# Three groups of tiles a round in a recurrence of layer norms and products, with results in single PSUM banks

## The chip, the cores and the metric

The kernel runs on one core of a Trainium2 chip. The metric is the time of one execution on the device, in microseconds (us). Three runs of the kernel before took 1946.14 to 1951.07 us, with a median of 1948.44. One further execution was recorded by the hardware profiler; every duration below is from that one.

The core's engines work side by side, each through its own list of instructions in order, and wait for one another by semaphores: TensorE (PE in the profile; PEld is its loading of weights), VectorE (DVE), ScalarE (ACT), GpSimd (POOL) and SyncE (SP), which issues DMAs. PE writes its results into PSUM. Its banks hold 512 float32 values a partition, and the kernel's pools use eight of them.

## The reference, cut to what matters

`x` has 3327 rows of 256 float32 features. Two layers follow each other, each a graph attention over a 3327 x 3327 adjacency and then a feed-forward part; every part takes a layer-normalized `x` and is added to `x`. The feed-forward part of layer 0 is a mixture of 16 experts, two of them for each row. That of layer 1 is a recurrence of 30 steps, and it is the part that the change touches:

```python
def step(h, _):
    h = h + 0.01 * jnp.tanh(h)
    h = h * jax.nn.sigmoid(h)
    h = _layernorm(h, ln_w, ln_b)
    h = jnp.einsum('bsc,dc->bsd', h, W) + b
    return (h, None)
x, _ = jax.lax.scan(step, x, None, length=N_ITERS)   # N_ITERS = 30
```

A row's next state depends on that row alone, and each step needs the one before.

## The kernel before, in words

The rows are held as 26 tiles of 128 rows in one SBUF tensor `x` (128 partitions x 26 x 256). The program has four stages: attention 0, whose products end at 391 us of the profile; the experts, from 395 us on; attention 1, whose products (L286) run from 793 to 1090 us; and the recurrence, whose first transpose is at 1090.1 us and whose last product starts at 1937.9 us. Results leave by DMA until the span ends at 1945.2 us.

In the recurrence the tiles form seven groups a step: six of four tiles and one of two. `x` holds the state times 100 (S). The layer norm is folded: `wc` is the weight matrix scaled by `ln_w`, with its mean taken out, so a product of the raw features gives the centred result; only the factor 1/sqrt(variance + eps) of each row (`rr`) is left to apply to the result, with the bias `bb`.

A list `parts` (L1080) has all 210 pairs of step and group in order. It is worked off in rounds of two parts (L1081 to L1084): first `turn_group` for both, then `next_state` for both.

`turn_group` (L1031): ScalarE computes tanh of a group's state (L1037, into `th`); GpSimd adds the state (L1039); ScalarE applies Silu (L1040, into `z`). For each tile VectorE takes the statistics (L1045), and PE transposes its two 128 x 128 halves (L1048) into a PSUM bank that holds two tiles (`pt`). The banks come from the pools `ps` and `ps_t` in turn, two banks each.

`next_state` (L1052): `inv_norm` (L1020) has VectorE aggregate the statistics (L1025) and GpSimd compute `rr` (L1027, L1028). ScalarE copies each bank of transposes to SBUF (L1058, `zT`). PE multiplies each tile with `wc`, two products a tile (L1063), into `po`, a PSUM tile for the whole group: 4 x 256 values, two banks; the pool has two such tiles, four banks. A second loop over the tiles has VectorE evict each one (L1069): result times `rr` plus `bb`, into `x`. In the last step a saved copy of the rows (`old`, from `kept`) is added (L1076) and the result goes out by DMA (L76).

What sets the order: transposes and products carry `tc.keep_in_program_order` and stand on PE as they are written. The rest of each engine's list is laid out by the framework's scheduler when the program is built, with the waits between engines set from the reads and writes of tiles; on the chip each list is followed in order. `th`, `z` and `zT` come from the pool `steps` with two buffers each; `stats`, `v` and `rr` from `small` with four.

Of the kernel before, what the change touches and what calls it, by code (L numbers as in the profile page):

```python
# [11 lines left out]
F32 = mybir.dt.float32  # L12
# [4 lines left out]
ALU = mybir.AluOpType  # L17
AX = mybir.AxisListType
PSUM = bass.MemoryType.PSUM

P = 128
# [4 lines left out]
G = 4  # L26
# [4 lines left out]
def gat_moe_gat_recurrent_ffn(ctx: ExitStack, tc: tile.TileContext, a: dict, out: bass.AP):  # L31
    nc = tc.nc
    N, D = a["x"].shape
# [30 lines left out]
    small = ctx.enter_context(tc.tile_pool(name="small", bufs=4))  # L64
# [3 lines left out]
    x = state.tile([P, NT, D], F32, name="x")  # L68
# [4 lines left out]
    def move_pairs(dram, tile, c0, c1, into_dram):  # L73

        def move(dst, src):
            nc.sync.dma_start(*((dst, src) if into_dram else (src, dst)))  # L76

        full = min(c1, PAIRS - 1)
        if full > c0:
            move(  # L80
                dram[c0 * 2 * P : full * 2 * P, :].rearrange("(t p b) d -> p t (b d)", p=P, b=2),
                tile[:, : 2 * (full - c0), :].rearrange("p (t b) d -> p t (b d)", b=2),
            )
        if c1 == PAIRS:
            base, last = (PAIRS - 1) * 2 * P, 2 * (PAIRS - 1 - c0)
            for r0, r1 in spread(REST // 2):
                move(
                    dram[base + 2 * r0 : base + 2 * r1, :].rearrange("(p b) d -> p (b d)", b=2),
                    tile[r0:r1, last : last + 2, :].rearrange("p b d -> p (b d)"),
                )  # L90
            if REST % 2:
                move(dram[base + REST - 1 : base + REST, :], tile[REST // 2 : REST // 2 + 1, last, :])
# [289 lines left out]
    with ExitStack() as moe:  # L382
# [5 lines left out]
        part = route_p.tile([P, 1], F32, name="part")  # L388
# [15 lines left out]
        ps = moe.enter_context(tc.tile_pool(name="ps0", bufs=4, space=PSUM))  # L404
        ps_o = moe.enter_context(tc.tile_pool(name="ps0o", bufs=2, space=PSUM))
# [240 lines left out]
        two = rec.tile([P, 2, SLOTS], F32, name="prod")  # L646
# [273 lines left out]
        wc = rec.tile([P, KD, D], F32, name="wc")  # L920
        bb = rec.tile([P, D], F32, name="bb")
# [15 lines left out]


    kept = dram.tile([NP, D], F32, name="kept")
    steps = ctx.enter_context(tc.tile_pool(name="steps", bufs=2))  # L940
    ps = ctx.enter_context(tc.tile_pool(name="ps2", bufs=2, space=PSUM))
    with ExitStack() as st:
        keep = st.enter_context(tc.tile_pool(name="keep2", bufs=1))
# [5 lines left out]
        ps_o = st.enter_context(tc.tile_pool(name="ps2o", bufs=2, space=PSUM))  # L949
# [62 lines left out]


    with ExitStack() as st:
        ps_t = st.enter_context(tc.tile_pool(name="ps3t", bufs=2, space=PSUM))
        turns = cycle((ps, ps_t))
        ps_o = st.enter_context(tc.tile_pool(name="ps3o", bufs=2, space=PSUM))
        last_p = st.enter_context(tc.tile_pool(name="last", bufs=2))

        def inv_norm(stats, n):  # L1020


            v = small.tile([P, G, 2], F32, name="v")
            for j in range(n):
                nc.vector.bn_aggr(v[:, j, :], stats[:, j, :])  # L1025
            r = small.tile([P, G], F32, name="rr")
            nc.gpsimd.tensor_scalar(r[:, :n], v[:, :n, 1], EPS, None, op0=ALU.add)  # L1027
            nc.gpsimd.tensor_tensor(r[:, :n], r[:, :n], neg_half[:, :n], ALU.pow)  # L1028
            return r

        def turn_group(ts):  # L1031

            n = len(ts)
            hs = x[:, ts[0] : ts[0] + n, :]
            th = steps.tile([P, G, D], F32, name="th")
            z = steps.tile([P, G, D], F32, name="z")
            nc.scalar.activation(th[:, :n, :], hs, AF.Tanh, scale=1.0 / S)  # L1037

            nc.gpsimd.tensor_tensor(th[:, :n, :], th[:, :n, :], hs, ALU.add)  # L1039
            nc.scalar.activation(z[:, :n, :], th[:, :n, :], AF.Silu, scale=1.0 / S)  # L1040
            stats = small.tile([P, G, 6], F32, name="stats")
            pool = next(turns)
            pt = [pool.tile([P, 2, KD, P], F32, name="bank") for _ in range(0, n, 2)]
            for j in range(n):
                nc.vector.bn_stats(stats[:, j, :], z[:, j, :])  # L1045
                for k in range(KD):
                    tc.keep_in_program_order(
                        nc.tensor.transpose(pt[j // 2][:, j % 2, k, :], z[:, j, k * P : (k + 1) * P], ident)  # L1048
                    )
            return pt, stats  # L1050

        def next_state(step, ts, pt, stats):  # L1052
            n = len(ts)
            hs = x[:, ts[0] : ts[0] + n, :]
            rr = inv_norm(stats, n)
            zT = steps.tile([P, G, KD, P], F32, name="zT")
            for c in range(n // 2):
                nc.scalar.copy(zT[:, 2 * c : 2 * c + 2, :, :], pt[c])  # L1058
            po = ps_o.tile([P, G, D], F32, name="po")
            for j in range(n):  # L1060
                for k in range(KD):
                    tc.keep_in_program_order(
                        nc.tensor.matmul(  # L1063
                            po[:, j, :], lhsT=zT[:, j, k, :], rhs=wc[:, k, :],
                            start=(k == 0), stop=(k == KD - 1),
                        )
                    )
            for j in range(n):
                nc.vector.scalar_tensor_tensor(  # L1069
                    x[:, ts[0] + j, :], po[:, j, :], rr[:, j : j + 1], bb, op0=ALU.mult, op1=ALU.add  # L1070
                )
            if step == N_STEPS - 1:
                here = slice(ts[0] * P, (ts[-1] + 1) * P)
                old = last_p.tile([P, G, D], F32, name="old")
                nc.sync.dma_start(old[:, :n, :], kept[here, :].rearrange("(t p) d -> p t d", p=P))
                nc.vector.scalar_tensor_tensor(hs, hs, 1.0 / S, old[:, :n, :], op0=ALU.mult, op1=ALU.add)  # L1076
                move_pairs(out, hs, ts[0] // 2, (ts[-1] + 1) // 2, True)


        parts = [(step, ts) for step in range(N_STEPS) for ts in groups]  # L1080
        for i in range(0, len(parts), 2):  # L1081
            two = [part + turn_group(part[1]) for part in parts[i : i + 2]]
            for part in two:
                next_state(*part)  # L1084


# [47 lines left out]
```

## Time and profile before

| | us |
|---|---|
| median of three runs | 1948.44 |
| profiled execution | 1946.91 |
| span of the profile, first to last instruction | 1945.2 |
| PE busy | 1899.3 |
| VectorE busy | 1278.6 |
| ScalarE busy | 1100.8 |
| GpSimd busy | 938.9 |
| products of the recurrence (L1063): 3120 passes, busy | 692.9 |
| transposes of the recurrence (L1048): 1560, busy | 187.7 |

The mean granted clock of PE is 0.994 of full speed.

How to read it. A line of the timeline has the start in us from the span's start, the time, the engine, the line of the kernel, the operation, output<-inputs, shapes and types, and how many instructions were merged (x32); in brackets stands the idle time of that engine just before and what ended it. A line of the costliest groups ends with the busy time of the group and the mean in ns of one, and behind the last bar the idle time ahead of the group. In the table of stretches each engine has its busy time and its number of instructions, and the last three columns are the granted clock of PE, the DMA share and the DMA rate. PE's products of float32 are two passes each, so 1560 products of the program stand as 3120. Passes are pipelined: the record of one overlaps the start of the next, so the pace is read from start to start. In a program's order, "waits DVE_49" on an instruction means that it waits for a count on VectorE's semaphore, "Activation_49" for one on ScalarE's.

### The profile page before, as it was taken

Reading aid. Unit: us, or ns where it says so; the run is one execution under the profiler, and the core shown is the slowest. Engines: PE = TensorE matmul, PEld = TensorE weight load, DVE = VectorE, ACT = ScalarE, POOL = GpSimd, SP = SyncE. Lnnn points to the kernel's source line nnn. Section 1 sums busy time; section 2 is a strip of 40 time slices with the busy share of each in tenths; the row PEclk is TensorE's granted clock in tenths of the full one; section 3 lists DMA queues with packets and bytes.
Section 4 is the critical chain, followed back from the end, with each engine's and each line's share of the span. In section 5 each row is a group of like instructions: output and inputs, shape, how many; then the busy total and the mean of one; then the engine's idle time right before and its main releaser. Section 6 shows DMA issues by size and latency. Waiting matters only on the chain.

```text
span 1945.2 us, 33722 instructions
## 1 busy us (share of the span) xinstructions
PE 1899.3 (98%) x11987; PEld 1745.9 (90%) x11987; DVE 1278.6 (66%) x3828; ACT 1100.8 (57%) x1593; POOL 938.9 (48%) x864
## 2 busy tenths in 40 slices
PE   7999999989999998999999999999999999999998
PEld 6999999989999996888888888888888888888887
DVE  6888788832222225477766777777777777777777
ACT  2977766721111112666655666666666666666664
POOL 3010202354333331001000488888888888888886
PEclk9999999999999998999999999999999999999999
DMA  8978051089999875000000100000000000000003
GB/s 170 120 104 116 10 86 51 18 295 292 350 336 335 290 249 174 9 21 13 18 20 11 36 1 1 1 1 1 1 1 1 1 1 2 1 1 1 1 1 119
DMA packets 140946, 158.61 MB, mean 82 GB/s; under 512 B 52168, under 2 KB 100555, under 8 KB 140777
## 3 DMA queue, kind: packets, MB, share of 16 engines
q1 hardware_dynamic: 124657, 123.57, 20.5%
q0 software_dynamic: 11440, 28.09, 8.4%
q10 hardware_dynamic: 4680, 4.76, 0.7%
q8 instruction: 98, 1.61, 0.3%
q14 instruction: 71, 0.58, 0.1%
HBM read 166.09 MB, written 29.80 MB: 101 GB/s over the span
## 4 chain that ended last, share of the span: by engine, by line
PE 72%; issue 9%; DVE 5%; POOL 5%; DMA 2%; ACT 0%; another core or an unknown queue 0%; SPq 0%; POOLq 0%; DVEq 0%; ACTq 0%
PE po L1063 35%; PE acc L286 23%; PE bank L1048 9%; POOL given L851 2%; DVE pT L281 2%; PE bank L831 2%; POOL rb L757 2%; DMA given<-wh,to 2%; PE acc L847 1%; PE acc L162 1%; PE bank L526 1%; POOL rstd L120 0%; PE bank L147 0%; DVE x L961 0%
## 5 line engine op out<-in xcount | busy, mean ns | idle before, releaser
L1063 PE MATMUL po<-wc,zT 128*128 128x256 f32 x3120 | 692.9, 380 | 0.0
L1063 PEld LDWEIGHTS po<-wc,zT 128*128 128x128 f32 x3120 | 585.3, 190 | 75.5
L1039 POOL TENSOR_TENSOR th<-th,x 128x1024 f32<-128x1024 f32 (+1 forms) x210 | 460.9, 2217 | 101.9 <-ACT th L1037 100.3
L276 ACT ACTIVATE e<-rb,minus,full 128x384 f32<-128x384 f32 (+3 forms) x494 | 400.4, 824 | 179.3 <-DVE pT L281 161.0
L281 DVE SCALAR_TENSOR_TENSOR pT<-e,part,adjT 128x384 f32<-128x384 f32 (+3 forms) x494 | 380.4, 774 | 131.9 <-PE acc L286 112.4
L1045 DVE BATCH_NORM_STATS2 stats<-z 128x6 f32<-128x256 f32 x780 | 273.9, 413 | 147.6 <-ACT z L1040 147.6
L1069 DVE SCALAR_TENSOR_TENSOR x<-po,rr,bb 128x256 f32<-128x256 f32 x780 | 321.0, 474 | 59.3 <-PE po L1063 57.5
L1058 ACT COPY zT<-bank 128x512 f32<-128x512 f32 x390 | 200.9, 599 | 270.2 <-PE bank L1048 270.2
L286 PE MATMUL acc<-wh,pT 128*128 128x129 f32 x2704 | 309.5, 276 | 1.6 <-DVE pT L281 1.6
L286 PEld LDWEIGHTS acc<-wh,pT 128*128 128x128 f32 x2704 | 305.0, 192 | 2.1 <-DVE pT L281 2.0
L286 PE MATMUL acc<-s_wh,pT 128*128 128x257 f32 x1352 | 296.1, 382 | 2.7 <-DVE pT L281 2.7
L286 PEld LDWEIGHTS acc<-s_wh,pT 128*128 128x128 f32 x1352 | 257.7, 191 | 40.9 <-DVE pT L281 4.8
L120 POOL TENSOR_TENSOR rstd<-ve,neg_half 128x4 f32<-128x4 f32 (+3 forms) x28 | 31.0, 1109 | 392.5 <-DVE ve L118 307.4
L1028 POOL TENSOR_TENSOR rr<-rr,neg_half 128x4 f32<-128x4 f32 (+1 forms) x210 | 209.2, 996 | 17.5
L1040 ACT ACTIVATE z<-th 128x1024 f32<-128x1024 f32 (+1 forms) x210 | 200.9, 1019 | 1.3 <-POOL th L1039 1.3
L1037 ACT ACTIVATE th<-x 128x1024 f32<-128x1024 f32 (+1 forms) x210 | 199.2, 1010 | 1.7 <-DVE x L127 1.7
L1048 PE MATMUL bank<-ident,z 128*128 128x128 f32 x1560 | 187.7, 273 | 1.6 <-DVE high L996 1.6
L1048 PEld LDWEIGHTS bank<-ident,z 128*128 128x128 f32 x1560 | 177.0, 141 | 12.4 <-ACT zT L1058 1.8
L881 DVE TENSOR_TENSOR pT<-e,bank 128x512 f32<-128x512 f32 x61 | 41.9, 687 | 183.2 <-PE bank L831 123.1
L831 PEld LDWEIGHTS bank<-hT,wh 128*128 128x128 f32 x1280 | 150.7, 194 | 8.3 <-ACT hT L823 6.4
L831 PE MATMUL bank<-hT,wh 128*128 128x128 f32 x1280 | 151.9, 278 | 5.8 <-ACT hT L823 5.8
L877 ACT ACTIVATE e<-bank 128x512 f32<-128x512 f32 x61 | 36.4, 597 | 189.6 <-issue 85.5
(192 smaller groups left out, 1331.7 us busy)
## 6 DMA issues: line engine op xcount, KB each, us to landing
wh<-in_w_dram SPq DMA_DIRECT2D x120, 512.0 KB
first_set<-in_w_dram SPq DMA_DIRECT2D x63, 512.0 KB
in_bytes<-in_adj_dram POOLq DMA_DIRECT2D x3, 2496.0 KB
x<-in_x_dram SPq DMA_DIRECT2D x6, 512.0 KB
kept<-x SPq DMA_DIRECT2D x8, 384.0 KB
old<-kept SPq DMA_DIRECT2D x6, 512.0 KB
out_dram<-x SPq DMA_DIRECT2D x6, 512.0 KB
table_x<-row ACTq DMA_DIRECT2D x3, 768.0 KB
```

The source lines that it names most:

```text
L276: nc.scalar.activation(e[:, : n * P], rb[:, : n * P], AF.Relu, scale=sc.full[:, j, h : h + 1], bias=sc.minus[:, j, h : h + 1],)
L281: masked = nc.vector.scalar_tensor_tensor(pT[:, : n * P], e[:, : n * P], sc.part[:, j, h : h + 1], adjT[:, j // 2, ts[0] * P : (ts[-1] + 1 ...
L286: nc.tensor.matmul(po[c], lhsT=pT[:, c * P : (c + 1) * P], rhs=wh[:, j, h, :], start=(j == 0 and c % per_bank == 0), stop=(j == NT - 1), s ...
L831: nc.tensor.matmul(p[:, f, :], lhsT=w[:, k, f * P : (f + 1) * P], rhs=hT[:, k, :], start=(k == 0), stop=(k == KD - 1),)
L1028: nc.gpsimd.tensor_tensor(r[:, :n], r[:, :n], neg_half[:, :n], ALU.pow)
L1039: nc.gpsimd.tensor_tensor(th[:, :n, :], th[:, :n, :], hs, ALU.add)
L1040: nc.scalar.activation(z[:, :n, :], th[:, :n, :], AF.Silu, scale=1.0 / S)
L1045: nc.vector.bn_stats(stats[:, j, :], z[:, j, :])
L1048: nc.tensor.transpose(pt[j // 2][:, j % 2, k, :], z[:, j, k * P : (k + 1) * P], ident)
L1058: nc.scalar.copy(zT[:, 2 * c : 2 * c + 2, :, :], pt[c])
L1063: nc.tensor.matmul(po[:, j, :], lhsT=zT[:, j, k, :], rhs=wc[:, k, :], start=(k == 0), stop=(k == KD - 1),)
L1069: nc.vector.scalar_tensor_tensor(x[:, ts[0] + j, :], po[:, j, :], rr[:, j : j + 1], bb, op0=ALU.mult, op1=ALU.add)
```

## The change

The recurrence takes three parts a round: three groups are turned, then all three have their products. 210 parts make 70 rounds. `steps` has three buffers; `ps_t` has four banks, and every second and third group takes its transposes' banks from it; `stats`, `v` and `rr` come from a pool `marks` of six. The results of the products go to PSUM tiles of two tiles, one bank each, of which there are two, and the eviction by VectorE stands in the same loop over the tiles as the products.

```diff
-    steps = ctx.enter_context(tc.tile_pool(name="steps", bufs=2))
+    steps = ctx.enter_context(tc.tile_pool(name="steps", bufs=3))
...
-        ps_t = st.enter_context(tc.tile_pool(name="ps3t", bufs=2, space=PSUM))
-        turns = cycle((ps, ps_t))
+        ps_t = st.enter_context(tc.tile_pool(name="ps3t", bufs=4, space=PSUM))
+        turns = cycle((ps, ps_t, ps_t))
         ps_o = st.enter_context(tc.tile_pool(name="ps3o", bufs=2, space=PSUM))
         last_p = st.enter_context(tc.tile_pool(name="last", bufs=2))
+        marks = st.enter_context(tc.tile_pool(name="marks", bufs=6))
...
-            v = small.tile([P, G, 2], F32, name="v")
+            v = marks.tile([P, G, 2], F32, name="v")
...
-            r = small.tile([P, G], F32, name="rr")
+            r = marks.tile([P, G], F32, name="rr")
...
-            stats = small.tile([P, G, 6], F32, name="stats")
+            stats = marks.tile([P, G, 6], F32, name="stats")
...
-            po = ps_o.tile([P, G, D], F32, name="po")
             for j in range(n):
+                if j % 2 == 0:
+                    po = ps_o.tile([P, 2, D], F32, name="po")
                 for k in range(KD):
                     tc.keep_in_program_order(
                         nc.tensor.matmul(
-                            po[:, j, :], lhsT=zT[:, j, k, :], rhs=wc[:, k, :],
+                            po[:, j % 2, :], lhsT=zT[:, j, k, :], rhs=wc[:, k, :],
                             start=(k == 0), stop=(k == KD - 1),
                         )
                     )
-            for j in range(n):
                 nc.vector.scalar_tensor_tensor(
-                    x[:, ts[0] + j, :], po[:, j, :], rr[:, j : j + 1], bb, op0=ALU.mult, op1=ALU.add
+                    x[:, ts[0] + j, :], po[:, j % 2, :], rr[:, j : j + 1], bb, op0=ALU.mult, op1=ALU.add
                 )
...
-        for i in range(0, len(parts), 2):
-            two = [part + turn_group(part[1]) for part in parts[i : i + 2]]
-            for part in two:
+        for i in range(0, len(parts), 3):
+            some = [part + turn_group(part[1]) for part in parts[i : i + 3]]
+            for part in some:
                 next_state(*part)
```

## The prediction

> **What bounds the kernel now.** I read the page's busy shares, the costliest groups and the chain that ended last; then the timeline of one round of the recurrence, engine by engine; then the order of both built programs. TensorE (PE) is busy 98% of the span, and the recurrence (first transpose 1090.1 us, last matmul 1937.9 us) is 44% of it.
>
> ```profile
> PE 1899.3 (98%) x11987; PEld 1745.9 (90%) x11987; DVE 1278.6 (66%) x3828; ACT 1100.8 (57%) x1593; POOL 938.9 (48%) x864
> ...
> L1063 PE MATMUL po<-wc,zT 128*128 128x256 f32 x3120 | 692.9, 380 | 0.0
> ...
> L1069 DVE SCALAR_TENSOR_TENSOR x<-po,rr,bb 128x256 f32<-128x256 f32 x780 | 321.0, 474 | 59.3 <-PE po L1063 57.5
> ```
>
> The products at L1063 have 0.0 us of idle time before them; VectorE (DVE) waits for them, not they for it. One eight-tile round on PE:
>
> ```profile
> 1408.36 7.07 PE L1063 MATMUL po<-wc,zT 128*128 128x256 f32 x32
> 1415.27 1.91 PE L1048 MATMUL bank<-ident,z 128*128 128x128 f32 x16
> 1417.02 1.03 PE L1063 MATMUL po<-wc,zT 128*128 128x256 f32 x4
> ```
>
> From 1408.36 to 1415.27 there are 32 product passes: 0.216 us each, four to a tile (each float32 product is two passes). The 16 transposes to 1417.02 are 0.109 each. A tile costs 4 x 0.216 + 2 x 0.109 = 1.08 us, 780 tiles make 842, and the recurrence takes 847 from its first transpose on. So PE is at its own pace here: all gaps together are some 5 us, and a change of order can't gain more than that. That is 0.26%; about 0.3% (5.8 us) is what a measurement of this kernel can tell from no change.
>
> **The change, part by part.** Against the profiled execution: 1946.9 us, span 1945.2, so 1.7 around it; the median of the runs shown, 1948.4, is 1.5 higher, and I add nothing for that.
>
> *Three groups a round.* 105 rounds become 70. A change from transposes to products costs PE nothing when enough transposes hide ScalarE's first copy. Rounds of six tiles have only 12, and there the first product waits: 29 such changes lose 0.07 us each, 2.1 us in all. Rounds of ten or twelve tiles have 20 or 24 transposes, so this goes: **-2.1 us**. No operation is added, so PE's 842 us stay.
>
> *The eviction moves into the product loop.* This decides. L1069 stood in a loop of its own, behind all products of a group; it now stands inside the loop over tiles, so a bank's first tile is evicted, in program order, ahead of the products of its second tile, which go into the same bank. The built program guards that. In its order on PE each bank of two tiles reads:
>
> ```
> L1065 Matmult po<-wc,zT 128x256 [waits Activation_49]
> L1065 Matmult po<-wc,zT 128x256
> L1065 Matmult po<-wc,zT 128x256 [waits DVE_49]
> L1065 Matmult po<-wc,zT 128x256
> ```
>
> In before, the four instructions stand together with one wait ahead of them. Counting VectorE's semaphore through the built program, the value awaited by the third instruction is the one that the eviction of the *first tile of the same bank* sets, in 390 banks of 390. So in every bank PE finishes tile 0, stops until VectorE has read it, and only then begins tile 1. All that is queued on PE stands behind it.
>
> The price, from rows of before. The first two lines give PE to VectorE; the others, from the attention, give VectorE to PE.
>
> ```profile
> 1399.84 0.38 PE L1063 MATMUL po<-wc,zT 128*128 128x256 f32 x1
> ...
> 1400.32 1.66 DVE L1069 SCALAR_TENSOR_TENSOR x<-po,rr,bb 128x256 f32<-128x256 f32 x4 [1.48 <-PE po L1063]
> ```
>
> ```profile
> 1070.93 0.47 DVE L281 SCALAR_TENSOR_TENSOR pT<-e,part,adjT 128x256 f32<-128x256 f32 x1
> ...
> 1071.45 0.48 PE L286 MATMUL acc<-s_wh,pT 128*128 128x257 f32 x1 [0.71 <-DVE pT L281]
> ```
>
> - The last pass of tile 0 is on record for 0.379 us, 0.163 beyond its 0.216 slot.
> - VectorE starts 0.107 after that record ends (1399.84 + 0.38 to 1400.32).
> - An eviction that had to wait lasts 0.483.
> - A PE that waits for VectorE starts 0.054 after its end (1071.40 to 1071.45).
> - That first pass is on record for 0.485, not 0.379 (0.48 against 0.38): 0.106 more, as its weights weren't loaded ahead. All five such rows of 256 or 257 columns at full clock, 502.48 to 1073.70, agree within 2 ns.
>
> Sum: 0.163 + 0.107 + 0.483 + 0.054 + 0.106 = 0.913 us for each bank. Nothing hides it. 390 banks (13 a step, 30 steps): **+356.1 us**. If the weights are loaded ahead after all it is 0.807 a bank and 314.7, the lower bound of this term.
>
> *Does VectorE get there at once?* Per bank PE now takes 8 x 0.216 + 0.913 = 2.64 us. VectorE has two evictions (0.392 apart when they follow each other), two statistics (0.327) and two aggregations (0.066): 1.57 us. It is in order, so what counts is what stands ahead of a tile-0 eviction. After one ends, the tile-1 eviction is due 0.054 + 0.106 + 0.863 (tile 1) + 0.27 (0.163 and 0.107 again) = 1.29 us later, and the next tile-0 eviction 0.86 after that began. In the built order at most four statistics (1.31 us) stand in the first space, one (0.33) in the second (0.47 free). They fit, barely. The factors rr come from GpSimd (POOL): per group 2.3 + 0.3 + 1.3 = 3.9 us, 11.7 a round; a round of 12 tiles now lasts 12 x 1.08 + 6 x 0.913 = 18.4. I take zero. The other bound: one statistics (0.33) ahead of each tile-0 eviction, 390 x 0.33 = +129.
>
> *Two banks in place of four for results.* A bank's next first tile needs its old second tile evicted, which VectorE did ahead of the eviction that PE has already waited for. Nothing, as long as the wait above stands. Without that wait VectorE would have 1.73 us for two evictions (0.78), and the blocks of statistics between would be in the way.
>
> *th, z, zT in three buffers, marks in six.* Memory, no instructions: nothing.
>
> *First and last rounds.* In before the first eviction came at 1097.76 and nobody waited. Now PE stands still for it. Its three groups are transposed by 1092.93 + 16 x 0.109 = 1094.7, its first tile is ready for VectorE at 1095.8, but in VectorE's order twelve statistics, the end of the attention and the scaling of x come first: about 9 us from 1091, then rr, so some 1100.8: **+5** (0 to +10). In the last step a 1.18 us sum (L1076) follows each group and holds up the next group's first eviction by some 0.75, four times: +3; the last sum no longer queues behind another of 1.2, and the tail shortens by 1.6: **+1.4**.
>
> 1946.9 - 2.1 + 356.1 + 5 + 1.4 = **2307 us**, 18% slower.
>
> *A rule of the skill at this place.* No row of before shows PE writing into a bank while VectorE reads another part of it. The Trainium skill, PSUM — Partial Sum Buffer, section "PSUM bank collisions raise a hardware error", says that engines have to be kept apart by bank, not by address: disjoint columns of one bank still collide. By a guard on addresses the third instruction would wait for nothing and the sum would be 1945; by the page's guard, the one in the built program, it is 2307.
>
> **The rivals.**
>
> 1. *The wait is met when PE gets there: no change.* It would have to be for an eviction further back. Then -2.1 is left: 1945, and 1942 at the very best, as gaps of 5 us are all there is to gain. It decides if VectorE's eviction ends less than 0.1 us after tile 0; against it stand the count of the semaphore and 0.48 us of eviction. This is the case on the other side: 3%, of which I give 1% to a time faster by over 0.3%, since 1942 lies near that line.
>
> 2. *Statistics in the way.* The static order was laid out for some assumed times; where VectorE runs later than that, each eviction PE waits for queues behind 0.33 us or more. At half of the banks: +64, 2371; at all: 2436. For it: 1.31 us in a space of 1.29. Against it: 1.1 us of each 2.64 is free on VectorE. 11%.
>
> 3. *PE's clock falls.* The clock changes in stretches of 3.41 us. Rows of before:
>
> ```profile
> 789.90:793.40 3.50, 1.69 (x11) 1.25 (x10) 1.76 (x5) 3.04 (x9) 0.00 (x0) 0.99 0.04 8
> 793.40:796.80 3.40, 3.40 (x9) 2.69 (x8) 1.46 (x3) 2.21 (x5) 0.00 (x0) 0.50 0.17 58
> 1090.30:1093.70 3.40, 1.78 (x16) 1.58 (x15) 2.96 (x9) 2.90 (x5) 0.00 (x0) 1.00 0.58 182
> ```
>
> A stretch with PE busy 1.69 of 3.50 (the figure behind the comma) was followed by half clock (0.50); one with 1.78 of 3.40 was not. In the new pattern PE is idle on record 0.644 of each 2.64 us, so at worst twice in a stretch: busy 2.12 of 3.41, above the row that kept its clock. If every other stretch fell, products and transposes would take a third longer: +280, 2590. The Trainium skill, TensorE: Matmul & The Clock Gate, section "A second HAM failure mode: psum-queue depth-cycling", tells of a kernel whose short idle times at PSUM made the clock swing; nothing here shows that at idle times below 1.4 us. 5%.
>
> **How the numbers follow.** Forecast as worked out 81%, rival 1 3%, rival 2 11%, rival 3 5%. Forecast 2307. Its own bounds are 2266 (0.807 a bank) and about 2345 (0.1 us of queueing a bank); the first contradicts five rows, so I go down to 2280. Up, the range takes in the nearer half of rival 2: 2385. Rival 3, rival 1 and the rest of 2 stay outside, under 2 in 10. Faster by over 0.3% 1%, within 0.3% 2%, slower 97%.
>
> **What the changed profile would show.** Right: PE idle before its products, released by VectorE's eviction, some 390 times of 0.64 us (250 us on record); evictions waiting for PE and starting 0.11 after the record of tile 0's last pass; rounds of twelve tiles 18.4 us apart, of ten 15.4; granted clock at 1.00; ScalarE and GpSimd with more idle time and the same work. Wrong: no PE idle time (rival 1), evictions that start later than 0.15 us after tile 0 with statistics just ahead of them (rival 2), a clock below 1.00 in the recurrence (rival 3).

## The result, and the profile after

The changed kernel takes **2304.84 us**, the median of 6 runs (2302.1 to 2305.7), against 1947.99 us, the median of 6 runs of before (1946.14 to 1951.07). The ratio is 1.1829, 95% interval 1.1817 to 1.184: 18% slower. The profiled execution took 2304.76 us, its span is 2303.1, and the mean granted clock is 0.994 as in before.

In the changed kernel the lines below the edited lists have moved: transposes stand at L1049, copies at L1059, products at L1065, evictions at L1070, statistics at L1046. The page of after, its busy shares and three of its costliest groups:

```profile
PE 2004.7 (87%) x11987; PEld 1714.1 (74%) x11987; DVE 1324.9 (58%) x3828; ACT 1110.2 (48%) x1593; POOL 930.9 (40%) x864
...
L1065 PE MATMUL po<-wc,zT 128*128 128x256 f32 x3120 | 791.0, 393 | 250.8 <-DVE x L1070 250.8
...
L1070 DVE SCALAR_TENSOR_TENSOR x<-po,rr,bb 128x256 f32<-128x256 f32 x780 | 375.2, 481 | 491.6 <-PE po L1065 479.2
...
L1046 DVE BATCH_NORM_STATS2 stats<-z 128x6 f32<-128x256 f32 x780 | 286.8, 413 | 23.1 <-ACT z L1041 22.2
```

The instruction counts of these engines are those of before, to the last one. The change adds no work. PE's share fell from 98% to 87%, and 250.8 us of idle time now stand ahead of the products, where before had 0.0; all of it ends with an eviction at L1070. In the other direction VectorE waits 479.2 us for the products. Each of the two waits for the other, in turn.

The waits of PE give the count (engine, tile and line, what it waited for, then us in total, times, longest):

```profile
PE po L1065 <- DVE x L1070: 250.8, 390, 5.2
```

390 waits: one for each of 13 banks in each of 30 steps. The timelines of after show one of them. First the products on PE from 1500.3 us, then VectorE over part of the same stretch:

```profile
1500.39 1.03 PE L1065 MATMUL po<-wc,zT 128*128 128x256 f32 x4
1502.06 1.99 PE L1065 MATMUL po<-wc,zT 128*128 128x256 f32 x8 [0.65 <-DVE x L1070]
1504.70 1.99 PE L1065 MATMUL po<-wc,zT 128*128 128x256 f32 x8 [0.65 <-DVE x L1070]
1507.28 1.99 PE L1065 MATMUL po<-wc,zT 128*128 128x256 f32 x8 [0.58 <-DVE x L1070]
```

```profile
1504.16 0.48 DVE L1070 SCALAR_TENSOR_TENSOR x<-po,rr,bb 128x256 f32<-128x256 f32 x1
1504.56 1.39 DVE L1046 BATCH_NORM_STATS2 stats<-z 128x6 f32<-128x256 f32 x4
1505.88 0.48 DVE L1070 SCALAR_TENSOR_TENSOR x<-po,rr,bb 128x256 f32<-128x256 f32 x1
1506.27 0.42 DVE L1046 BATCH_NORM_STATS2 stats<-z 128x6 f32<-128x256 f32 x1
1506.73 0.48 DVE L1070 SCALAR_TENSOR_TENSOR x<-po,rr,bb 128x256 f32<-128x256 f32 x1
```

An x8 on PE is no longer two tiles of one bank: it is the second tile of one bank and the first tile of the next. Behind each such eight PE stops. The eight from 1504.70 end on record at 1506.69; VectorE evicts from 1506.73 to 1507.21; PE goes on at 1507.28. Between two evictions that PE waits for, VectorE finds room for four statistics, the other tile's eviction and one more statistic.

Busy times over 400 us in the middle of the recurrence (start:end and length, then PE, PEld, DVE, ACT and POOL, granted clock, DMA share, GB/s), before and then after:

```profile
1300.00:1700.00 400.00, 400.00 (x2218) 359.39 (x2217) 299.36 (x1109) 269.34 (x383) 335.81 (x300) 1.00 0.00 1
```

```profile
1300.00:1700.00 400.00, 318.58 (x1569) 244.38 (x1570) 228.68 (x796) 194.18 (x269) 239.52 (x216) 1.00 0.00 1
```

In the same 400 us PE goes through 1569 instructions in place of 2218, at the same clock. ScalarE, GpSimd and VectorE do less because they are fed less.

Where the 357.9 us of added span lie: from the recurrence's first transpose to its last product 1202.47 us in place of 847.65 (+354.8); the recurrence begins 5.1 us later (1095.4 in place of 1090.3), in stages that the change doesn't edit; from the start of the last product to the end of the span it is 5.2 in place of 7.2 (-2.0).

### The profile page after: what moved, and what is told of

It reads as the page before. It is cut to its first block, busy times and chain, and to the rows that moved or that the text cites. A ratio compares the mean times of both kernels' runs of the same rounds, so it can differ in the third digit from the quotient of the medians.

```text
span 2303.1 us, 33505 instructions
## 1 busy us (share of the span) xinstructions
PE 2004.7 (87%) x11987; PEld 1714.1 (74%) x11987; DVE 1324.9 (58%) x3828; ACT 1110.2 (48%) x1593; POOL 930.9 (40%) x864
## 4 chain that ended last, share of the span: by engine, by line
PE 51%; DVE 17%; ACT 11%; issue 10%; POOL 4%; DMA 2%; another core or an unknown queue 0%; DVEq 0%; POOLq 0%; SPq 0%; ACTq 0%
PE po L1065 24%; PE acc L286 20%; DVE x L1070 9%; ACT zT L1059 8%; DVE stats L1046 4%; ACT z L1041 3%; DVE pT L281 2%; POOL given L851 2%; PE bank L831 2%; POOL rb L757 2%; PE bank L1049 2%; DMA given<-wh,to 1%; PE acc L162 1%; PE acc L847 1%; DVE v L1026 1%
## 5 line engine op out<-in xcount | busy, mean ns | idle before, releaser
L1065 PE MATMUL po<-wc,zT 128*128 128x256 f32 x3120 | 791.0, 393 | 250.8 <-DVE x L1070 250.8
L1065 PEld LDWEIGHTS po<-wc,zT 128*128 128x128 f32 x3120 | 556.2, 190 | 464.9 <-DVE x L1070 407.7
L1070 DVE SCALAR_TENSOR_TENSOR x<-po,rr,bb 128x256 f32<-128x256 f32 x780 | 375.2, 481 | 491.6 <-PE po L1065 479.2
L1038 ACT ACTIVATE th<-x 128x1024 f32<-128x1024 f32 (+1 forms) x210 | 210.2, 1007 | 345.4 <-DVE x L1070 293.1
L1059 ACT COPY zT<-bank 128x512 f32<-128x512 f32 x390 | 197.7, 610 | 269.7 <-PE bank L1049 269.7
L286 PE MATMUL acc<-wh,pT 128*128 128x129 f32 x2704 | 309.5, 275 | 1.6 <-DVE pT L281 1.6
L286 PEld LDWEIGHTS acc<-wh,pT 128*128 128x128 f32 x2704 | 305.0, 192 | 2.1 <-DVE pT L281 2.0
L286 PE MATMUL acc<-s_wh,pT 128*128 128x257 f32 x1352 | 297.1, 382 | 4.0 <-DVE pT L281 3.9
L1046 DVE BATCH_NORM_STATS2 stats<-z 128x6 f32<-128x256 f32 x780 | 286.8, 413 | 23.1 <-ACT z L1041 22.2
L286 PEld LDWEIGHTS acc<-s_wh,pT 128*128 128x128 f32 x1352 | 257.1, 191 | 43.7 <-DVE pT L281 7.4
L1049 PE MATMUL bank<-ident,z 128*128 128x128 f32 x1560 | 181.9, 273 | 1.8 <-DVE high L996 1.8
L1049 PEld LDWEIGHTS bank<-ident,z 128*128 128x128 f32 x1560 | 174.7, 141 | 9.1 <-ACT low L997 2.0
L881 DVE TENSOR_TENSOR pT<-e,bank 128x512 f32<-128x512 f32 x61 | 41.9, 687 | 182.0 <-PE bank L831 121.8
```

Source lines behind the costliest of these rows:

```text
L286: nc.tensor.matmul(po[c], lhsT=pT[:, c * P : (c + 1) * P], rhs=wh[:, j, h, :], start=(j == 0 and c % per_bank == 0), stop=(j == NT - 1), s ...
L1065: nc.tensor.matmul(po[:, j % 2, :], lhsT=zT[:, j, k, :], rhs=wc[:, k, :], start=(k == 0), stop=(k == KD - 1),)
L1070: nc.vector.scalar_tensor_tensor(x[:, ts[0] + j, :], po[:, j % 2, :], rr[:, j : j + 1], bb, op0=ALU.mult, op1=ALU.add)
```

## The experiments

**My theory** was the prediction's: one wait a bank, of about 0.9 us, set because an eviction stands in program order between two products into the same PSUM tile; everything else in the change is worth a few us. **The rivals**: the smaller result buffers (two banks in place of four) or the three groups a round carry part of the loss; the guard is set by something other than the PSUM tile, such as the bank; VectorE's order adds to the wait. And one question on the other side: are the three groups worth anything if the wait goes?

**Take the wait away, keep everything else.** After, with both evictions of a bank behind both of its products.

```diff
-                nc.vector.scalar_tensor_tensor(
-                    x[:, ts[0] + j, :], po[:, j % 2, :], rr[:, j : j + 1], bb, op0=ALU.mult, op1=ALU.add
-                )
+                if j % 2 == 1:
+                    for i in (j - 1, j):
+                        nc.vector.scalar_tensor_tensor(
+                            x[:, ts[0] + i, :], po[:, i % 2, :], rr[:, i : i + 1], bb, op0=ALU.mult, op1=ALU.add
+                        )
```

> The changed kernel, but both evictions of a bank stand behind both its products. Three groups a round, two banks of results, all buffers stay. Theory: the wait inside a bank is gone; a bank is used again after one other bank, 1.73 us, in which VectorE needs 0.27 + 2 x 0.392 + 0.09 + 0.05 = 1.2. If few statistics stand ahead of the pairs, 1945 (the 2 us of waits for ScalarE's copies gained); up to 2050 if a block of three or four stands ahead of most pairs. Rival (two banks are too few, or three groups cost): 2150 or more, most of the loss stays.

Measured 1953.17 us (1949.75 to 1955.43), ratio to before 1.0033 (1.002 to 1.0047). Its waits of PE, and then its products and evictions in the timelines of PE and of VectorE:

```profile
PE po L1065 <- DVE x L1072: 3.4, 2, 3.1
```

```profile
1500.07 10.56 PE L1065 MATMUL po<-wc,zT 128*128 128x256 f32 x48
```

```profile
1502.44 0.86 DVE L1072 SCALAR_TENSOR_TENSOR x<-po,rr,bb 128x256 f32<-128x256 f32 x2
1503.22 1.07 DVE L1046 BATCH_NORM_STATS2 stats<-z 128x6 f32<-128x256 f32 x3
1504.20 0.86 DVE L1072 SCALAR_TENSOR_TENSOR x<-po,rr,bb 128x256 f32<-128x256 f32 x2
```

The 48 passes of a twelve-tile round run through in one piece, and the evictions come in pairs. With the three groups, the single banks and the two result buffers all in place, 352 us of the loss are gone. What is left is some 6 us above before: the products lose 7.5 us between them in this run (before: 3.1), 3.3 of it in the first round and most of the rest in short waits, and the recurrence begins 1.6 us later. The waits that six-tile rounds no longer have (2 us) don't make up for that.

**Move the eviction alone.** Before, with its two groups and its `po` of four tiles in two banks, and only the second loop's head removed, so that the eviction stands in the product loop.

```diff
-            for j in range(n):
                 nc.vector.scalar_tensor_tensor(
```

> The kernel before with one edit: the eviction stands inside the product loop. Two groups a round and four banks for results stay. Theory (PE stops after a tile until that tile is evicted, wherever the next products go to the same PSUM tile): in the built program not only the second but each of tiles 1, 2 and 3 of a group waits here for the eviction just before it, also tile 2, which lies in the other bank. That is 19 waits a step, 570 in all. In the changed kernel such a wait costs 0.913 us where the eviction waits for PE and for rr (a group's first) and 0.843 where it waits for PE alone: 210 x 0.913 + 360 x 0.843 = 495, so 2442 us. If only the wait inside a bank cost something, 390 x 0.88 = 343 and 2291. Rival (three groups a round or the two banks are what costs): no loss, 1948.

Measured 2468.99 us (2464.71 to 2472.14), ratio 1.2679 (1.2657 to 1.27). Its waits of PE:

```profile
PE po L1063 <- DVE x L1068: 361.2, 555, 1.8
...
PE po L1063 <- DVE v L1025: 10.0, 15, 0.7
```

555 and 15 are 570: in each step, 19 of the 26 tiles wait, that is every tile of a group but its first. The third tile of a group waits as well, although it goes to the other bank and nobody has touched that. **What is guarded is the PSUM tile of the program, not the bank.** That is a matter of how the framework sets waits, and it is why the loss of after is smaller than that of its main edit made alone. The time came out 27 us above what I expected: the products lose 525.5 us in place of 3.1, which is 0.917 us a wait. Most of the surplus is in one place, the 180 waits of a group's third tile: they cost 0.952 us on average in place of the 0.843 expected, 20 us in all. That tile waits for VectorE and for ScalarE's copy of its transposes, the wait for VectorE stands in a separate instruction on PE, and in all 180 PE starts 0.146 us after the eviction ends, in place of 0.055. And in 75 of them VectorE is late for the eviction, nearly always behind a statistic, 9 us in all. (The aggregations at L1025, to which the profile puts 15 waits down, follow the eviction and hold nothing up: the 0.146 is the same there.)

The Trainium skill, PSUM — Partial Sum Buffer, section "PSUM bank collisions raise a hardware error", asks for a guard by bank and quadrant. The guard in this program goes further than that where a tile spans two banks: 570 waits here, 390 where each tile is a bank (next run). What the chip does without the guard was not tried.

**The same with single banks, still two groups.** Before, with `po` tiles of one bank (four of them) and the eviction in the loop.

```diff
-        ps_o = st.enter_context(tc.tile_pool(name="ps3o", bufs=2, space=PSUM))
+        ps_o = st.enter_context(tc.tile_pool(name="ps3o", bufs=4, space=PSUM))
...
-            po = ps_o.tile([P, G, D], F32, name="po")
             for j in range(n):
+                if j % 2 == 0:
+                    po = ps_o.tile([P, 2, D], F32, name="po")
...
-            for j in range(n):
                 nc.vector.scalar_tensor_tensor(
...
```

> The kernel before, two groups a round, with results in tiles of one bank (four of them) and the eviction inside the product loop. It differs from the run with the eviction alone moved (2469 us) only in that a group's result is two PSUM tiles in place of one. Theory (the framework guards a PSUM tile as a whole, so the wait follows the tile and not the bank): tile 2 of a group no longer waits for the eviction of tile 1; 390 waits as in the changed kernel in place of 570, at the 0.917 that one cost there 2304, at the 0.88 of the changed kernel 2291. So within 1% of the changed kernel, although rounds have two groups and there are four banks. Rival (the number of groups or banks carries a part of the loss): well away from 2305, or still near 2469.

Measured 2294.85 us (2294.03 to 2296.0), ratio 1.1781 (1.1762 to 1.18).

```profile
PE po L1064 <- DVE x L1069: 244.4, 390, 1.5
```

390 waits again, with two groups a round and four result banks. Neither the number of groups nor that of the banks carries the loss. Against the run before this one, 180 waits fewer took away 174 us. The 10 us to after come mostly from the start: PE's longest wait is 1.5 us here and 5.2 there, and after begins its recurrence later.

**Single banks, evictions behind the bank, two groups, four banks.** As the run above, with the evictions placed as in the first experiment.

```diff
-            for j in range(n):
-                nc.vector.scalar_tensor_tensor(
-                    x[:, ts[0] + j, :], po[:, j, :], rr[:, j : j + 1], bb, op0=ALU.mult, op1=ALU.add
-                )
+                if j % 2 == 1:
+                    for i in (j - 1, j):
+                        nc.vector.scalar_tensor_tensor(
+                            x[:, ts[0] + i, :], po[:, i % 2, :], rr[:, i : i + 1], bb, op0=ALU.mult, op1=ALU.add
+                        )
```

> The kernel before, two groups a round, results in tiles of one bank (four of them), both evictions of a bank behind both its products. No wait inside a bank, four banks, so a bank is used again after three others (5.2 us): nothing to wait for. Theory: 1946, as before; evictions start a bank earlier, so the tail after the last product may be 1 us shorter. It would be the fastest of these versions, by less than can be measured. Rival (single banks cost something by themselves): over 1953, as with three groups and two banks.

Measured 1950.07 us (1946.22 to 1953.1), ratio 1.001 (1.0001 to 1.002). The products lose 3.0 us, and the recurrence takes 847.64 from first transpose to last product, as in before. An eviction that comes earlier, a bank at a time, is worth nothing: PE doesn't wait for evictions in before. The end was expected 1 us shorter and is 2.5 longer, 9.8 us behind the start of the last product in place of 7.2: in this run's order the evictions of the last group of four wait for `rr` until 1938.82 us.

**A bank for every tile.** After, with one result tile of one bank for each tile, of which half is used; the eviction stays in the loop.

```diff
-                if j % 2 == 0:
-                    po = ps_o.tile([P, 2, D], F32, name="po")
+                po = ps_o.tile([P, 2, D], F32, name="po")
...
-                            po[:, j % 2, :], lhsT=zT[:, j, k, :], rhs=wc[:, k, :],
+                            po[:, 0, :], lhsT=zT[:, j, k, :], rhs=wc[:, k, :],
...
```

> The changed kernel, but each tile's result has a bank of its own; the eviction stays inside the product loop, just as in the changed kernel. Two banks, so a tile waits for the eviction two tiles back. Theory (what costs is the shared bank, not the place in the loop): 0.863 us of products against 0.27 + 0.48 + 0.05 = 0.80 for the eviction, so no wait if VectorE is free, 0.27 for each statistics that stands ahead of an eviction; the built order has one or two between evictions for about a third of the tiles: 1945 to 2080, say 2000. Rival (the place in the loop costs, whatever the bank): 2300.

Measured 2006.67 us (2004.57 to 2008.06), ratio 1.0306 (1.029 to 1.0321). The place of the eviction in the loop is the same as in after, and 298 us of the loss are gone: now a tile waits for the eviction of the tile *two* before it, and the products of the tile between hide 0.86 us of that. The latency they have to hide is 0.163 + 0.107 + 0.483 + 0.054 = 0.81, so 0.05 is to spare, and one statistic (0.33) ahead of an eviction uses it up: the products lose 61.1 us, 4.6 of it in one wait of the first round and most of the rest in some 610 passes, at about 380 tiles, that start 0.02 to 0.3 us late. So two banks with one tile each are nearly enough, but not quite; three were not tried.

**The other bank's product between.** After, with a group's tiles in the order 0, 2, 1, 3 over two banks, so that a tile's eviction has another bank's products beside it.

```diff
-            for j in range(n):
-                if j % 2 == 0:
-                    po = ps_o.tile([P, 2, D], F32, name="po")
+            po = [ps_o.tile([P, 2, D], F32, name="po") for _ in range(0, n, 2)]
+            for j in (0, 2, 1, 3)[:n] if n == 4 else range(n):
...
```

> The changed kernel with the order of a group's products turned to tile 0, tile 2, tile 1, tile 3: the two banks in alternation, the eviction still inside the loop, the wait inside each bank still there. Theory (the wait is a latency of 0.84 to 0.91 us that one tile of other products, 0.863, can lie beside): what stays is 0.05 us at the 360 waits of the groups of four, more where a statistics stands ahead of an eviction, and the full 0.91 at the 30 groups of two: 1947 + 18 + 27 = 1992, up to 2040. That is the case of one bank for each tile (2007) over again, with the groups of two added. Rival (PE loses its time at each change of bank or by pieces of two products): 2300.

Measured 2026.08 us (2024.37 to 2028.04), ratio 1.0417 (1.04 to 1.0434). Its waits of PE:

```profile
PE po L1064 <- DVE x L1069: 26.2, 34, 4.4
```

34 long waits are left in place of 390: 30 of them are in the groups of two tiles, which have one bank only and no other product to put between; the others are one in the first round and three in the last step. Together the products lose 85.2 us; some 53 of that, as in the run above, are late starts too short to be listed there. The price of the wait is the same latency in all of these; what differs is how much of it another bank's products cover.

**Make the wait longer by a known amount.** After, with a statistic over a bank's first tile in PSUM added ahead of its eviction; nobody uses its result.

```diff
+                if j % 2 == 0:
+                    extra = marks.tile([P, 6], F32, name="extra")
+                    nc.vector.bn_stats(extra, po[:, 0, :])
```

> The changed kernel with one instruction more: VectorE takes the statistics of each bank's first tile, straight from its bank, just ahead of evicting it; nothing uses them. Theory (VectorE's time between the two tiles stands on PE's path in full): 390 x 0.327 = 127 more, less up to 13 where the wait for PE and that for GpSimd now stand on two instructions: 2420 to 2435. Rival (the wait is mostly fixed cost of the semaphores, VectorE's work lies beside it): within 30 us of 2305.

Measured 2415.2 us (2413.27 to 2417.29), ratio 1.2418 (1.2397 to 1.2439): 110 us above after, a little under what I expected. Its waits of PE, and two instructions of VectorE's timeline (PE's eight passes before them end on record at 1502.59):

```profile
PE po L1065 <- DVE x L1073: 365.7, 390, 5.2
```

```profile
1502.63 0.43 DVE L1072 BATCH_NORM_STATS2 extra<-po 128x6 f32<-128x256 f32 x1
1502.98 0.47 DVE L1073 SCALAR_TENSOR_TENSOR x<-po,rr,bb 128x256 f32<-128x256 f32 x1
```

365.7 is 114.9 more than in after, 0.295 us for each of 390 banks, where one statistic takes 0.33 of VectorE. So nearly all of what VectorE does between product and eviction goes into the time: the loop PE to VectorE to PE is the bound of every bank. The missing 0.03 has a reason that is taken up below.

**Three groups alone.** Before, with three groups a round, three buffers in `steps`, the pool `marks`, and the copies of the transposes moved into `turn_group`; `po` and its evictions as in before. (The place of the copies differs from after's, so this is not a clean cut of the change.)

```diff
-    steps = ctx.enter_context(tc.tile_pool(name="steps", bufs=2))
+    steps = ctx.enter_context(tc.tile_pool(name="steps", bufs=3))
...
+            zT = steps.tile([P, G, KD, P], F32, name="zT")
+            for c in range(n // 2):
+                nc.scalar.copy(zT[:, 2 * c : 2 * c + 2, :, :], pt[c])
+            return zT, stats
...
-        for i in range(0, len(parts), 2):
-            two = [part + turn_group(part[1]) for part in parts[i : i + 2]]
+        for i in range(0, len(parts), 3):
+            some = [part + turn_group(part[1]) for part in parts[i : i + 3]]
```

> The kernel before with three groups a round and nothing else of the change: four banks for results, evictions in a loop of their own, four banks for transposes; ScalarE's copies are issued with the transposes, so that the third group's transposes can use the first's banks again. Theory: 1945, the 2 us at the rounds of six tiles gained, and PE's pace as it was; a few us more if the third group's transposes wait for the copies. Rival (three groups a round are themselves slower, as states are due sooner): over 1960.

Measured 1963.51 us (1962.69 to 1964.79), ratio 1.0087 (1.0073 to 1.0102). I had expected no change; this is 17 us slower, as the rival had it. Its waits of PE in the recurrence:

```profile
PE po L1064 <- DVE x L1070: 6.5, 10, 0.7
...
PE bank L1049 <- ACT zT L1053: 2.3, 9, 0.3
```

What PE waits for are buffers. With two `po` tiles of two banks for three groups, the third group's results go where the first's were; where a group of two tiles stands in the middle, PE comes back after 1.73 us of products, and the first group's four evictions have not ended: ten waits of 0.8 us from start to start. One of them on PE, then VectorE before it:

```profile
1497.52 2.83 PE L1064 MATMUL po<-wc,zT 128*128 128x256 f32 x12 [0.65 <-DVE x L1070]
```

```profile
1493.42 2.38 DVE L1046 BATCH_NORM_STATS2 stats<-z 128x6 f32<-128x256 f32 x7 [2.23 <-ACT z L1041]
1495.73 2.42 DVE L1070 SCALAR_TENSOR_TENSOR x<-po,rr,bb 128x256 f32<-128x256 f32 x6
```

Right behind the products, four evictions and the way there and back would make 0.27 + 3 x 0.392 + 0.48 + 0.05 = 1.98 us, a wait of 0.25. Here they begin 0.75 us behind the products and not 0.27, in all ten cases, as seven statistics stand ahead of them that have waited 2.23 us for ScalarE's `z`. The nine others are the third group's transposes, whose banks ScalarE hasn't copied yet. These two account for some 12 us of the recurrence's 13 (860.7 in place of 847.7), the later start for 3. PE waits nowhere for a state, so the rival's reason, states that are due sooner, is not shown as it was meant; but ScalarE's `z` comes late for VectorE, and that holds up the evictions. Whether three groups do this or the copies, which this run puts ahead of `z` on ScalarE, is open.

Nothing that was run is faster than before.

## Why the prediction was right

**The mechanism.** The third instruction of each bank waits for the eviction of the bank's first tile, 390 times: shown by the waits of after, by their going when the eviction moves behind the bank (1953), and by their coming with the eviction's place alone (2469 and 2295). The prediction took the guard for one by bank. In after a PSUM tile is one bank, so its count of 390 came out the same; that the guard goes by PSUM tile was found only by the run with 570 waits. The idle time on record was announced as 390 x 0.64 us, 250 in all; it is 250.8, in part by the luck told below.

**The price of one wait: one term was mis-sized.** From start to start, four of the five terms measured as predicted: the end of the record, the eviction that had to wait (median 0.483 us), VectorE to PE (0.054 to 0.056), and the first pass behind a wait (0.483 in 389 of 390 rows; the other, 0.794, is at half clock). The fifth, PE to VectorE, was taken as 0.107 for all. It is 0.107 or 0.108 in 203 of the 210 banks that come first in a group, but 0.038 or 0.039 in 141 of the 180 that come second, which makes 0.07 x 180 = 13 us less. This is the difference between 0.65 and 0.58 in the timeline above. The 0.107 came from a group's first eviction, which waits for PE and for GpSimd's `rr`; its wait for PE stands in a separate wait instruction in front of it. The eviction of a group's third tile waits for PE alone and carries that wait itself. The run with the second reader confirms it: its added statistic carries its own wait for PE in every bank and starts 0.04 behind the record, and so a bank that had 0.107 loses 0.33 - 0.07 = 0.26 in place of 0.33. 390 x 0.33 - 210 x 0.07 = 114, and 114.9 was measured. A row that showed the shorter value stood in before, in another stage: there L850 mostly starts 0.038 or 0.039 after the products it waits for, L881, and L1069 where it had to wait, mostly 0.106 to 0.108. L850 waits for a DMA too, but there the separate instruction holds the wait for the DMA, and L850 carries the one for PE; so what counts is where the wait for PE stands, and not how many engines are waited for. I took the one row that had the same line.

**VectorE gets there in time:** right. In the timeline above four statistics fit into the space that I had called barely enough, and rival 2 (2371 to 2436) did not come, but for a trace: a statistic just ahead makes the eviction start at 0.07 in 29 of the second banks and at 0.26 in 10, and two first banks start at 0.46. That is some 4 us.

**First round:** right in size. These are the timelines of VectorE and PE in after:

```profile
1105.73 0.48 DVE L1070 SCALAR_TENSOR_TENSOR x<-po,rr,bb 128x256 f32<-128x256 f32 x1 [1.28 <-POOL rr L1029]
```

```profile
1100.00 1.03 PE L1065 MATMUL po<-wc,zT 128*128 128x256 f32 x4
1106.27 3.78 PE L1065 MATMUL po<-wc,zT 128*128 128x256 f32 x8 [5.25 <-DVE x L1070]
1110.84 1.35 PE L1065 MATMUL po<-wc,zT 128*128 128x256 f32 x5 [0.79 <-DVE x L1070]
```

PE stands for 5.25 us, 4.6 more than in an ordinary bank, against the +5 predicted. The 3.78 of the eight passes behind it is 1.8 more than 1.99: the clock fell, see below.

**Last step:** right. The sum of 1.2 us at L1077 holds up the next eviction; four waits are 1.57 and three times 1.37 in place of 0.65, which makes 3.1 (predicted 3), and the tail is 2.0 shorter (predicted 1.6).

**Rounds of six tiles:** right. Before loses 2.2 us at the first products behind its transposes, after nothing. But for the first and the last step, rounds of twelve tiles start 18.3 to 18.5 us before the next and rounds of ten 15.25 (announced 18.4 and 15.4).

**Not foreseen:** the recurrence begins 5.1 us later. Over the recorded runs its start lies anywhere between 1089.4 and 1095.4. Of the 5.1 us, 3.4 have come about before the second attention's products (L286) begin, at 796.5 us in place of 793.1; the ten profiles have this start between 792.7 and 796.7, with two groups and with three alike. The other 1.7 lie within those products. With three groups there are six loads of ScalarE's tables around them in place of four; that can bear on the 1.7 at most, as the run with the second reader has six too and begins its recurrence at 1091.4, and two runs with four at 1091.3 and 1091.8. The cause stays open.

So the close hit, 2304.8 for 2307, is in part luck, errors that cancel: the waits were put 13 us too high, and the later start (5.1), the statistics ahead of evictions (4) and the slow clock after the first round (1.8) were not in the sum.

**The rivals.** "No change" was wrong: the waits are there and aren't met when PE gets there. "The clock falls" was wrong but for one place. These are stretches of after, the granted clock being the third figure from the end:

```profile
1100.40:1103.81 3.41, 0.63 (x3) 0.20 (x2) 3.41 (x14) 3.38 (x5) 0.71 (x1) 1.00 0.22 75
1103.81:1107.22 3.41, 0.95 (x2) 0.84 (x3) 2.13 (x17) 1.91 (x3) 2.71 (x5) 0.50 0.01 2
1107.22:1110.63 3.41, 2.83 (x7) 1.69 (x5) 3.41 (x11) 0.00 (x0) 2.29 (x3) 0.50 0.00 0
```

A stretch with PE busy 0.63 of 3.41 us is followed by two at half clock, 6.8 us in all. The ordinary stretches of the recurrence have PE busy for about 80% and keep 1.00. That agrees with the rows of before that the prediction went by. A single long wait isn't needed: where the eviction alone was moved (2469 us) PE never waits for more than 1.8 us in the recurrence, and yet one stretch at its start and one at its end were followed by half clock. This is the first, with waits of 0.88 and 0.84 us in it, and the stretch behind it:

```profile
1095.39:1098.80 3.41, 1.69 (x8) 0.87 (x6) 3.23 (x11) 3.36 (x6) 0.00 (x0) 1.00 0.15 49
1098.80:1102.20 3.40, 2.82 (x6) 1.83 (x7) 1.98 (x9) 3.39 (x4) 2.54 (x4) 0.50 0.22 77
```

So the price of rival 3 did not come, but what it describes happens where PE waits more.

The Trainium skill, TensorE: Matmul & The Clock Gate, section "A second HAM failure mode: psum-queue depth-cycling", tells of a kernel in which short idle times of PE between groups of products, often enough repeated, made the clock swing; it doesn't say how short. Here 390 of them, nearly all 0.58 to 0.65 us and one every 2.6 us, did not do so; the two falls in the run above, with 570, are the nearest to it. For these kernels the measurement decides.

## What to carry to other kernels

Before moving an eviction into the loop of products, look in the built order at what it then stands between: if the next product writes the same PSUM tile, PE waits for VectorE once per eviction, and the price is the whole way there and back (0.85 to 0.91 us here), not the eviction's 0.48, unless products into another PSUM tile lie between. The place that cost nothing was behind the bank's last product, with four result banks (1950); with two it was 1953. And an engine that is busy without gaps at its own pace, here PE with 5 us of gaps in 847, has no more than those gaps to gain from a new order of the work around it.

## What the runs showed of the hardware that was not expected

- An instruction of VectorE whose wait for PE stands in a separate wait instruction ahead of it starts 0.07 us later than one that carries that wait itself: 0.107 against 0.038 us after PE's record ends. On PE the same showed in the run with 570 waits: 0.146 against 0.055 us after the eviction ends.
- A stretch of 3.41 us with PE busy for 0.63 of it, in a wait of 5.2 us at the start of a stage, was followed by 6.8 us at half clock; the eight products behind it took 1.8 us longer. In another run one with PE busy for 1.69, around waits of 0.88 and 0.84 us, was followed by half clock as well.
- The framework's guard follows the program's PSUM tile: with a tile over two banks, PE waited for a reader in the bank it didn't write to, 180 times more than with one bank a tile, for 174 us.
